# Layer 1's softmax sums: half of the queries added on GpSimd, the other half added later on DVE

## The chip, the cores and the metric

The kernel runs on one core of one Trainium2 chip. The metric is the device time of that core in microseconds (us), for the whole batch of eight samples. Engines are named as in the profile: PE is TensorE (PEld is its weight load), DVE is VectorE, ACT is ScalarE, POOL is GpSimd, SP is SyncE, whose queue issues the DMAs.

## The reference

Two attention blocks run one after the other on x of shape (8, 512, 32, 32), in f32. Layer 0 has eight heads and a group norm, layer 1 one head over all 512 channels and a norm over the whole sample. Layer 1, which is what the change touches, cut to what matters:

```python
n = (x - mean) * rsqrt(var + eps) * gamma + beta      # over c, h, w
q, k, v = wq @ n + bq, wk @ n + bk, wv @ n + bv        # (512, 1024) each
attn = softmax(einsum('bci,bcj->bij', q, k) * c ** (-0.5))   # 1024 queries x 1024 keys
out = einsum('bcj,bij->bci', v, attn)
return x + wo @ out + bo
```

## The kernel before

Each sample is worked off by itself: `layer0`, then `attention1`. The order on PE, ACT and DVE is the order in which the program is written (a manual schedule for these three engines); GpSimd and the DMA queue also follow that order as far as their own instructions go. Most matrix products are made in the Strassen-Winograd form, with seven products of quarters instead of eight, so that DVE has many additions of quarters: operands (names S1..S4 of the left side, T1..T4 of the right side) and results (a product in PSUM added to what is in SBUF).

`together(...)` runs several such products in turn, one step of each at a time, and `at_steps(steps, hooks)` puts extra work behind step n. So a hook's number sets where its instructions stand in the queues of DVE and ACT.

The scores of layer 1 are a matrix of 1024 keys by 1024 queries, held transposed in eight tiles `ps[j][k][i]`: j is the half of the keys, i the half of the queries, and k counts the two 256-key groups in a half. A tile is 128 partitions by 1024 f32 and holds two rows of 512 queries (index u). The scores go through two levels of Strassen-Winograd. At the outer level there are seven products: three (A11·B11, S2·T2, S3·T3) are made directly, by `line(t)` for each of four groups of 128 keys, and four are halved again by `twice(...)`: the local names are `p5`, `p2`, and then, in the last stage, the pair of `S4`·`B22` (queries half 0, keys half 1) and `A22`·`T4` (queries half 1, keys half 0). I call these two p3 and p4. Each `twice` has seven steps, each of one PE group of four 128x256 matmuls, and two PSUM banks, `line` and `single`: steps 1, 3, 5 and 7 write `line`, steps 2, 4 and 6 `single`. After each step DVE adds the bank to SBUF (`add`, L1143), or ACT copies it. Where the product is final, ACT takes the exponential of the finished quarter (`exp_of`, L1106).

The three stages of the scores stand in the code in this order:

1. `at_steps(together(line(0), p5, line(1), p5), {})`
2. `at_steps(together(line(2), p2, line(3), p2), {...})`, with hooks: `with_p5` (L1187) adds an outer product to a tile, `c22(k)` does this for tile `ps[1][k][1]` and takes its exponential, and `halve_a`, `halve_b` (L1036, L1044) make the operands for p4.
3. `with_p5(0, 1, 1)`, and p3 and p4 together, with `c22(1)` behind step 2.

The softmax denominators are sums of the exponentials over the keys. `add_up` adds the rows of the tiles of query half i into `acc[:, i, :]`, seven 128x512 additions for each half (L1101 the first, L1103 the others). In the kernel before each of them stands on DVE straight behind the exponential that it reads. Later `sums` (L1302) adds the partitions of `acc` by a matmul with ones, DVE takes the reciprocal, and a DMA spreads it.

Then `values(0)` and `values(1)` make the product with v in the Strassen-Winograd form over seven steps. `finish_values(n)` (L1233, L1237) makes operands S_n and T_n on DVE: n = 1 ahead of the first step, the others behind steps 1, 3 and 5; `sums` stands behind step 2. The first two products of each of `values(0)` and `values(1)` (A11·B11 and A12·B21) need no such operands.

PSUM has two buffers of tag `s` and two of tag `o`, which all these stages share in turn, so that a product can begin only when DVE or ACT has read what the last user of its buffer left.

Of the kernel before, what the change touches and what calls it, by code (L numbers as in the profile page):

```python
# [39 lines left out]
ALU = mybir.AluOpType  # L40
# [25 lines left out]
def two_attention_blocks(  # L66
# [17 lines left out]
    nc = tc.nc  # L84
# [13 lines left out]
    def banks(tag, name):  # L98
        return psum.tile([P, 2, HALF], FP, tag=tag, name=name)

    def tile2(name):
        return tpool.tile([P, 2, HALF], FP, tag="t", name=name)
# [351 lines left out]
    def together(*groups):  # L454

        groups = list(groups)
        spares.clear()
        while groups:
            for g in list(groups):
                if next(g, g) is g:  # L460
                    groups.remove(g)
                else:
                    yield
        spares.clear()

    def at_steps(steps, hooks):

        n = -1
        for n, _ in enumerate(steps):
            for hook in hooks.get(n, []):  # L470
                hook()
        assert n >= max(hooks, default=-1)
# [202 lines left out]
    def flat(t):  # L675
        return t.rearrange("p h n -> p (h n)")
# [322 lines left out]
    def attention1(xs, norm, b, at_values):  # L999
# [19 lines left out]
        def halve(part, order):  # L1019

            quarter = {}
            for i in range(2):
                for j in range(2):
                    k, n = order(i, j)
                    quarter[f"{i + 1}{j + 1}"] = part[:, k, n * 2 * P : (n + 1) * 2 * P]
            return quarter

        def halve_a(name):
            q = {f"A{n}": v for n, v in halve(q_parts[name], lambda i, j: (j, i)).items()}
            t = flat(tile2(f"{name}_twice_{b}"))  # L1030
            q.update({f"S{n + 1}": t[:, n * 2 * P : (n + 1) * 2 * P] for n in range(4)})
            for n, x, y, op in [
                (1, "A21", "A22", ALU.add), (2, "S1", "A11", ALU.subtract),
                (3, "A11", "A21", ALU.subtract), (4, "A12", "S2", ALU.subtract),
            ]:
                nc.vector.tensor_tensor(q[f"S{n}"], q[x], q[y], op)  # L1036
            twice_a[name] = q

        def halve_b(name):
            q = {f"B{n}": v for n, v in halve(bs[name], lambda i, j: (i, j)).items()}  # L1040
            t = flat(tile2(f"{name}_twice_{b}"))
            q.update({f"T{n + 1}": t[:, n * 2 * P : (n + 1) * 2 * P] for n in range(4)})
            for n, x, y in [(1, "B12", "B11"), (2, "B22", "T1"), (3, "B22", "B12"), (4, "B21", "T2")]:
                nc.vector.tensor_tensor(q[f"T{n}"], q[x], q[y], ALU.subtract)  # L1044
            twice_b[name] = q
# [48 lines left out]
        ps = [[[tile2(f"p_1_{b}_{j}{k}{i}") for i in range(2)] for k in range(2)] for j in range(2)]  # L1094
        acc = tile2(f"acc_1_{b}")
        seen = [[], []]

        def add_up(i, p):
            seen[i].append(p)
            if len(seen[i]) == 2:  # L1100
                nc.vector.tensor_tensor(acc[:, i, :], *seen[i], ALU.add)  # L1101
            elif len(seen[i]) > 2:
                nc.vector.tensor_tensor(acc[:, i, :], acc[:, i, :], p, ALU.add)  # L1103

        def exp_of(p):
            nc.scalar.activation(p, p, AF.Exp, scale=norm.factor)  # L1106

        def line(t):


            bank = banks("s", f"ps_s_1_{b}_{t}")[:, 0, :]
            for a, v, to in [
                ("A11", "B11", ps[0][t // 2][0]), ("S2", "T2", ps[1][t // 2][0]),
                ("S3", "T3", ps[0][t // 2][1]),
            ]:
                for k in range(2):
                    nc.tensor.matmul(  # L1117
                        bank, bs[v][:, k, t * P : (t + 1) * P], q_parts[a][:, k, :],
                        start=a == "A11" and k == 0, stop=k == 1, skip_group_check=True,
                    )  # L1120
                nc.scalar.copy(to[:, t % 2, :], bank)
                yield

        def twice(a, v, tags, i, j, fresh, final):

            a, v = twice_a[a], twice_b[v]
            line, single = (banks(tag, f"ps_{n}_1_{b}_{i}{j}")[:, 0, :] for tag, n in zip(tags, "ls"))

            def multiply(bank, x, y, start):
                for u in range(2):
                    nc.tensor.matmul(  # L1133
                        bank[:, u * 2 * P : (u + 1) * 2 * P], v[y][:, u * P : (u + 1) * P], a[x],
                        start=start and u == 0, stop=True, skip_group_check=True,
                    )

            def at(r, t):
                return ps[j][t][i][:, :, r * 2 * P : (r + 1) * 2 * P]

            def add(bank, r, t):
                bank = bank.rearrange("p (u q) -> p u q", u=2)
                nc.vector.tensor_tensor(at(r, t), bank, at(r, t), ALU.add)  # L1143

            def take(bank, r, t):
                if fresh:
                    nc.scalar.copy(at(r, t), bank.rearrange("p (u q) -> p u q", u=2))
                else:
                    add(bank, r, t)

            def done(r, t):
                if final:
                    exp_of(at(r, t))
                    if (r, t) in ((0, 1), (1, 0)):
                        for u in range(2):
                            add_up(i, ps[j][t][i][:, u, :])

            multiply(line, "A11", "B11", True)
            take(line, 0, 0)
            yield  # L1160
            multiply(single, "A12", "B21", True)
            add(single, 0, 0)
            done(0, 0)
            yield
            multiply(line, "S2", "T2", False)
            take(line, 0, 1)
            yield
            multiply(single, "S1", "T1", True)
            take(single, 1, 1)
            yield  # L1170
            multiply(line, "S3", "T3", False)
            add(line, 1, 1)
            done(1, 1)
            yield
            multiply(single, "S4", "B22", False)
            add(single, 0, 1)
            done(0, 1)
            yield
            multiply(line, "A22", "T4", False)
            take(line, 1, 0)  # L1180
            done(1, 0)
            yield

        def with_p5(i, j, k):

            to, other = ps[j][k][i], ps[1][k][1] if i == 0 else ps[0][k][1]
            nc.vector.tensor_tensor(to, to, other, ALU.add)  # L1187

        def c22(k):
            with_p5(1, 1, k)  # L1190
            exp_of(ps[1][k][1])
            for u in range(2):
                add_up(1, ps[1][k][1][:, u, :])

        p5 = twice("S1", "T1", "oo", 1, 1, True, False)
        at_steps(together(line(0), p5, line(1), p5), {})
        p2 = twice("A12", "B21", "oo", 0, 0, False, True)
        at_steps(together(line(2), p2, line(3), p2), {
            0: [lambda: with_p5(0, 1, 0)], 2: [lambda: c22(0)],
            6: [lambda: halve_a("A22")], 8: [lambda: halve_b("T4")],  # L1200
        })
        with_p5(0, 1, 1)
        at_steps(together(
            twice("S4", "B22", "so", 0, 1, False, True), twice("A22", "T4", "so", 1, 0, False, True)
        ), {2: [lambda: c22(1)]})

        tps = {f"T{n}": [tile2(f"t{n}_p_1_{b}_{k}") for k in range(2)] for n in range(1, 5)}
# [17 lines left out]
        def finish_values(n):  # L1225

            for k in range(2):
                a, b, a21, b12 = v_parts[k], p_parts[k], vs[k][:, :, 2 * P :], ps[0][k][1]
                x, y, op = {
                    1: (a21, a["A22"], ALU.add), 2: (a["S1"], a["A11"], ALU.subtract),  # L1230
                    3: (a["A11"], a21, ALU.subtract), 4: (a["A12"], a["S2"], ALU.subtract),
                }[n]
                nc.vector.tensor_tensor(a[f"S{n}"], x, y, op)  # L1233
                x, y = {
                    1: (b12, b["B11"]), 2: (b["B22"], b["T1"]), 3: (b["B22"], b12), 4: (b["B21"], b["T2"]),
                }[n]
                nc.vector.tensor_tensor(b[f"T{n}"], x, y, ALU.subtract)  # L1237
# [70 lines left out]
            invs.append(spread(invs[0], HD, lambda i: [(i, r) for r in range(2)], f"1_{b}"))  # L1308

        finish_values(1)  # L1310
        hooks = {n * 2 - 3: [lambda n=n: finish_values(n)] for n in range(2, 5)}
        hooks[5].extend([lambda: later.pop(0)()] * 2)
        hooks[2], hooks[6] = [sums], []
# [532 lines left out]
```

## Time and profile before

| | us |
|---|---|
| median of 3 runs | 2971.13 (2969.62 to 2971.99) |
| span of the profiled run | 2969.2 |
| PE busy | 2901.0 (98%) |
| DVE busy | 1944.7 (65%) |
| ACT busy | 1110.3 (37%) |
| POOL busy | 21.0 (1%), 28 instructions |
| mean granted PE clock | 0.986 of full speed |

PE is busy nearly all the time, so time can only go where PE idles (68.2 us of the span) or where it runs at less than its full clock. The busy share of PE says nothing of the second: a matmul at half the clock counts as busy for twice the time. The eight samples are alike; their periods are 365.2 us. The first samples' score stages begin near 320 and 686 us, the third's at 1051 us, and it is this third one that is read below.

### The profile page before, as it was taken

How to read it: one execution, taken by the hardware profiler on the slowest of the kernel's cores; microseconds unless marked ns; L12 is line 12 of the kernel's file. 1: busy time of each engine (PE TensorE's matmuls, PEld its weight loads, DVE VectorE, ACT ScalarE, POOL GpSimd, SP SyncE). 2: the span in 40 equal slices, each digit the busy share in tenths (PEclk: the TensorE clock that was granted, in tenths of full speed). 3: DMA queues.
4: the chain of work that ended last, by engine and by line, in shares of the span. 5: the costliest groups of instructions: out<-in, count | busy, mean ns of one | idle time of the engine just before them, and what ended most of it. 6: DMA issues, size and time to landing. Idle time of an engine off the chain costs nothing.

```text
span 2969.2 us, 35729 instructions
## 1 busy us (share of the span) xinstructions
PE 2901.0 (98%) x14480; PEld 1452.6 (49%) x14480; DVE 1944.7 (65%) x2580; ACT 1110.3 (37%) x1536; POOL 21.0 (1%) x28
## 2 busy tenths in 40 slices
PE   9999999999999999999999999999999999999998
PEld 6434654346533565335553355533555336553364
DVE  5676565765667656676566765677656775647846
ACT  3462314623155231552216522265222642226431
POOL 0000000000000000000000000000000000000000
PEclk9999999999999999999999999999999999999999
DMA  8412122220221203212032120322203222021001
GB/s 272 148 42 72 48 92 89 47 88 26 92 93 44 89 25 115 70 45 87 25 117 75 45 80 25 117 75 57 92 1 117 76 75 75 15 87 56 8 1 37
DMA packets 77661, 210.87 MB, mean 71 GB/s; under 512 B 19888, under 2 KB 20656, under 8 KB 71088
## 3 DMA queue, kind: packets, MB, share of 16 engines
q1 hardware_dynamic: 77344, 208.48, 22.1%
q8 instruction: 115, 1.88, 0.3%
q14 instruction: 58, 0.48, 0.1%
q10 hardware_dynamic: 144, 0.02, 0.0%
HBM read 137.43 MB, written 28.57 MB: 56 GB/s over the span
## 4 chain that ended last, share of the span: by engine, by line
PE 94%; DVE 4%; ACT 1%; issue 0%; POOL 0%; DVEq 0%; POOLq 0%
PE s L716 15%; PE ps_o L735 15%; PE ps_o L1245 14%; PE ps_q L479 13%; PE ps_v L494 13%; PE ps_k L479 7%; PE ps_p L479 6%; PE ps_s L1117 6%; PE ps_l L1133 2%; PE ps_s L1133 2%; DVE acc L1103 2%; DVE p L1143 1%; ACT p L1106 1%; DVE p L1187 1%; PE ps_wvo L596 0%; PE ps_wqk L626 0%
## 5 line engine op out<-in xcount | busy, mean ns | idle before, releaser
L645 ACT ACTIVATE p<-s 128x1024 f32<-128x1024 f32 x512 | 523.8, 1025 | 322.3 <-PE s L716 309.9
L647 DVE TENSOR_TENSOR acc<-acc,p 128x1024 f32<-128x1024 f32 x384 | 469.3, 1222 | 103.4 <-ACT p L645 92.0
L716 PE MATMUL s<-q,k 64*64 64x512 f32 x4096 | 531.5, 590 | 0.0
L735 PE MATMUL ps_o<-p,v 64*64 64x512 f32 x4096 | 528.7, 589 | 0.0
L716 PEld LDWEIGHTS s<-q,k 64*64 64x64 f32 x4096 | 154.0, 133 | 288.9 <-issue 266.0
L735 PEld LDWEIGHTS ps_o<-p,v 64*64 64x64 f32 x4096 | 156.6, 133 | 282.8 <-issue 278.0
L528 DVE TENSOR_TENSOR v<-ps_v,u_v 128x512 f32<-128x512 f32 x96 | 66.2, 690 | 164.4 <-PE ps_v L494 111.7
L421 ACT COPY u_v<-ps_v 128x512 f32<-128x512 f32 x96 | 56.3, 586 | 303.9 <-PE ps_v L494 295.3
L1245 PE MATMUL ps_o<-t_p,s_v 128*128 128x512 f32 x384 | 168.2, 594 | 0.0
L1245 PE MATMUL ps_o<-p,v 128*128 128x512 f32 x256 | 133.1, 686 | 31.2 <-DVE p L1143 31.2
L421 ACT COPY u_q<-ps_q 128x512 f32<-128x512 f32 x96 | 55.9, 582 | 250.3 <-PE ps_q L479 250.3
L1106 ACT ACTIVATE p<-p,factor 128x512 f32<-128x512 f32 (+1 forms) x112 | 87.2, 783 | 164.5 <-DVE p L1143 160.5
L647 DVE TENSOR_TENSOR acc<-p,p 128x1024 f32<-128x1024 f32 x64 | 77.9, 1217 | 84.6 <-ACT p L645 84.6
L1117 PE MATMUL ps_s<-s_q,t 128*128 128x512 f32 x256 | 120.3, 592 | 0.0
L1245 PEld LDWEIGHTS ps_o<-t_p,s_v 128*128 128x128 f32 x384 | 72.3, 190 | 94.5 <-issue 87.3
L479 PE MATMUL ps_q<-t,w_wqk 128*128 128x512 f32 x256 | 116.0, 597 | 0.0
L1143 DVE TENSOR_TENSOR p<-ps_l,p 128x512 f32<-128x512 f32 x104 | 69.8, 686 | 70.6 <-PE ps_l L1133 70.6
L479 PE MATMUL ps_p<-t_p,w_p 128*128 128x512 f32 x256 | 114.3, 595 | 0.6 <-DVE inv L658 0.5
L494 PE MATMUL ps_v<-w_wvo,t 128*128 128x256 f32 x512 | 113.1, 379 | 0.0
L856 DVE RECIPROCAL inv<-inv 128x512 f32<-128x512 f32 x28 | 93.7, 3346 | 22.9 <-ACT inv L654 22.9
L1245 PEld LDWEIGHTS ps_o<-p,v 128*128 128x128 f32 x256 | 56.0, 223 | 104.9 <-issue 104.9
L1143 DVE TENSOR_TENSOR p<-ps_s,p 128x512 f32<-128x512 f32 x88 | 59.9, 687 | 71.1 <-PE ps_s L1133 71.1
(318 smaller groups left out, 4043.8 us busy)
## 6 DMA issues: line engine op xcount, KB each, us to landing
x<-in_x SPq DMA_DIRECT2D x92, 512.0 KB, 7.2
w_qk<-stored_qk SPq DMA_DIRECT2D x14, 1792.0 KB, 7.2
inv<-inv SPq DMA_DIRECT2D x248, 64.0 KB, 2.0
w_wqk<-stored_wqk SPq DMA_DIRECT2D x8, 1792.0 KB, 8.2
fold<-acc SPq DMA_DIRECT2D x56, 256.0 KB, 3.1
w_wvo<-stored_wvo SPq DMA_DIRECT2D x8, 1792.0 KB, 7.7
out<-x SPq DMA_DIRECT2D x28, 512.0 KB, 2.8
w_v<-stored_v SPq DMA_DIRECT2D x7, 1792.0 KB, 7.0
```

The source lines that it names most:

```text
L421: nc.scalar.copy(us[n][:, :width], line[:, :width])
L479: nc.tensor.matmul(bank, w[a][:, k, c * P : (c + 1) * P], bs[b][:, k, :], start=fresh and k == 0, stop=k == 1, skip_group_check=True,)
L494: nc.tensor.matmul(bank[:, u * 2 * P : (u + 1) * 2 * P], bs[b][:, k, n * P : (n + 1) * P], w[a][:, k, :], start=fresh and u == k == 0, sto ...
L645: nc.scalar.activation(p, s, AF.Exp, scale=factor)
L647: nc.vector.tensor_tensor(acc, first, p, ALU.add)
L716: nc.tensor.matmul(s[cols, j, :], flat(ks[pair])[rows, k0 : k0 + HD], qs[pair][rows, g, :], start=True, stop=True,)
L735: nc.tensor.matmul(o[cols, half, :], vs[kt][rows, c0 : c0 + HD], p[rows, j, :], start=kt == 0, stop=kt == NT - 1,)
L1106: nc.scalar.activation(p, p, AF.Exp, scale=norm.factor)
L1117: nc.tensor.matmul(bank, bs[v][:, k, t * P : (t + 1) * P], q_parts[a][:, k, :], start=a == "A11" and k == 0, stop=k == 1, skip_group_check ...
L1133: nc.tensor.matmul(bank[:, u * 2 * P : (u + 1) * 2 * P], v[y][:, u * P : (u + 1) * P], a[x], start=start and u == 0, stop=True, skip_group ...
L1143: nc.vector.tensor_tensor(at(r, t), bank, at(r, t), ALU.add)
L1245: nc.tensor.matmul(bank, v_parts[kt // 2][a][:, kt % 2, c * P : (c + 1) * P], p_parts[kt // 2][b][:, kt % 2, cols], start=fresh and kt == ...
```

## The change

`add_up` gets the tile's indices in place of a row, and the engine is chosen by the half of the queries: half 0 on GpSimd, straight behind the exponentials as before; half 1 on DVE, but no longer behind the exponentials. One of its four tiles is added behind step 10 of stage 2, the other three after `finish_values(1)`, ahead of the first product with v. Further, in stage 2 the hooks move up: `c22(0)` from step 2 to 1, `halve_a("A22")` from 6 to 4, `halve_b("T4")` from 8 to 6, and `with_p5(0, 1, 1)` goes from behind the stage into its step 8. The order on PE is the same, instruction by instruction. The purpose is that DVE doesn't wait for exponentials between the additions for which PE waits.

```diff
-        def add_up(i, p):
-            seen[i].append(p)
-            if len(seen[i]) == 2:
-                nc.vector.tensor_tensor(acc[:, i, :], *seen[i], ALU.add)
-            elif len(seen[i]) > 2:
-                nc.vector.tensor_tensor(acc[:, i, :], acc[:, i, :], p, ALU.add)
+        def add_up(j, k, i):
+
+            engine = nc.vector if i else nc.gpsimd
+            for u in range(2):
+                seen[i].append(ps[j][k][i][:, u, :])
+                if len(seen[i]) == 2:
+                    engine.tensor_tensor(acc[:, i, :], *seen[i], ALU.add)
+                elif len(seen[i]) > 2:
+                    engine.tensor_tensor(acc[:, i, :], acc[:, i, :], seen[i][-1], ALU.add)
...
-                    if (r, t) in ((0, 1), (1, 0)):
-                        for u in range(2):
-                            add_up(i, ps[j][t][i][:, u, :])
+                    if i == 0 and (r, t) in ((0, 1), (1, 0)):
+                        add_up(j, t, i)
...
             exp_of(ps[1][k][1])
-            for u in range(2):
-                add_up(1, ps[1][k][1][:, u, :])
...
-            0: [lambda: with_p5(0, 1, 0)], 2: [lambda: c22(0)],
-            6: [lambda: halve_a("A22")], 8: [lambda: halve_b("T4")],
+            0: [lambda: with_p5(0, 1, 0)], 1: [lambda: c22(0)], 4: [lambda: halve_a("A22")],
+            6: [lambda: halve_b("T4")], 8: [lambda: with_p5(0, 1, 1)], 10: [lambda: add_up(1, 0, 1)],
         })
-        with_p5(0, 1, 1)
...
         finish_values(1)
+        for j, k in [(1, 1), (0, 1), (0, 0)]:
+            add_up(j, k, 1)
```

## The prediction

> **What bounds the kernel now.** I first read the page's busy shares (PE 98%), then the list of waits for PE alone, because only what makes PE wait can be worth anything. It is short:
>
> ```profile
> PE ps_o L1245 <- DVE p L1143: 31.2, 8, 3.9
> PE ps_l L1133 <- DVE p L1143: 20.0, 8, 2.5
> PE ps_s L1133 <- DVE p L1143: 9.8, 8, 2.7
> ```
>
> That is 61.0 of PE's 68.2 us of idle time: three waits per sample (2.5, about 1.2, and 3.9 us), all for DVE's additions of score products. Next, the table of stages for the third sample: stages 1 and 2 of the scores; stage 3; the first four products with v; the rest of those; everything else of the period.
>
> ```profile
> 1051.20:1083.90 32.70, 32.70 (x105) 19.77 (x105) 12.68 (x21) 11.76 (x19) 0.00 (x0) 1.00 0.15 56
> 1083.90:1105.80 21.90, 14.50 (x57) 11.49 (x57) 17.09 (x26) 6.96 (x10) 0.00 (x0) 0.89 0.00 1
> 1105.80:1122.30 16.50, 16.49 (x33) 7.18 (x34) 7.54 (x10) 2.51 (x4) 0.00 (x0) 0.84 0.00 0
> 1122.30:1158.00 35.70, 35.70 (x86) 15.47 (x85) 30.84 (x37) 6.70 (x12) 0.00 (x0) 1.00 0.33 104
> 1158.00:1416.40 258.40, 258.40 (x1512) 124.73 (x1512) 172.42 (x222) 109.27 (x144) 2.42 (x2) 1.00 0.25 77
> ```
>
> The columns are stretch, length, busy time of PE, PEld, DVE, ACT, POOL, and then PE's clock. Everywhere but in the second and third row PE is busy throughout at clock 1.00. In stage 3 it is busy for 14.50 of 21.90 us, at 0.89, and in the next row, where it doesn't wait, the clock is 0.84. So each stall costs twice: the wait, and a slow time after it. The weight loads show the slow time directly, at the start of the values and a little later:
>
> ```profile
> 1106.80 0.34 PEld L1245 LDWEIGHTS ps_o<-p,v 128*128 128x128 f32 x1 [0.52 <-issue]
> 1107.65 0.34 PEld L1245 LDWEIGHTS ps_o<-p,v 128*128 128x128 f32 x1 [0.52 <-issue]
> ...
> 1111.99 0.19 PEld L1245 LDWEIGHTS ps_o<-p,v 128*128 128x128 f32 x1 [0.24 <-issue]
> 1112.42 0.19 PEld L1245 LDWEIGHTS ps_o<-p,v 128*128 128x128 f32 x1 [0.24 <-issue]
> ```
>
> One every 0.85 us, then one every 0.43: half speed until 1111.5. Last, the chain of waits says what DVE does while PE stands:
>
> ```profile
> 1099.36 0.70 DVE p L1143
> 1100.06 0.02 issue
> 1100.08 0.73 ACT p L1106
> 1100.81 0.02 issue
> 1100.84 0.70 DVE acc L1103
> 1101.54 0.02 issue
> 1101.56 0.69 DVE acc L1103
> 1102.26 0.61 DVE p L1143
> ```
>
> An addition, its exponential, two sums that wait for it (0.78 us in which DVE stands), and only then the next addition, that PE needs. This round takes 2.8 us; PE makes the group for the next addition in 0.86.
>
> **What the Trainium skill says.** (1) "TensorE: Matmul & The Clock Gate", Part 1 (the HAM clock gate): PE drops to half its clock after an idle window of about 3.4 us and needs about as long a busy one to return; the windows run freely. The trace agrees in kind: half speed behind the 2.5 and 3.9 us waits, none behind the 1.0 us wait. (2) "SBUF — State Buffer", "Who interferes with whom": a DVE instruction with two SBUF inputs contends with a GpSimd instruction that reads SBUF, and the second to issue waits for the first; one with a single SBUF input doesn't. No run here shows it yet, GpSimd being idle at this place. (3) "GPSIMD Engine Reference", 3.1: a GpSimd f32 add of two tensors of 2048 elements takes 4497 ns, 1.96 times DVE's.
>
> **The change, part by part.**
>
> *The sums leave stage 3.* DVE's timeline has the 14 sums of this sample at 0.69 us each: one in stage 2 (1073.75), nine in stage 3 (1084.75 to 1105.1), four behind it. The nine go, 6.2 us, and with them DVE's waits for their exponentials (0.79 us each where the line of ACT is free, 1.21 at 1093.53). What stays is 14 additions at a pitch of 0.60 us (two back to back: 1084.75 to 1085.35) and one `with_p5` at 1.14: 9.5 us, against 14 PE groups x 0.86 = 12.04 us. So DVE becomes the faster of the two, and PE should run through. I walked it by hand with the delays of the trace: an addition starts 1.06 us after its PE group (1082.20 to 1083.26), and PE resumes 0.06 us after an addition (1089.98 to 1090.04).
>
> The last two groups of p2 start at 1082.20 and 1083.06, as before; additions at 1083.26 and 1084.12. p3 and p4 then start a group every 0.86 us from 1083.93. Additions: p3's first at 1084.99, p4's first 1085.85, p3's second 1086.71, then `with_p5(1, 1, 1)` 1087.31 to 1088.54, p4's second 1088.45 to 1089.14. PE needs: for p3's third group (1087.38) p3's first addition, ended 1085.68; for p4's third (1088.24) 1086.54; for p3's fourth (1089.10) 1087.40; for p4's fourth (1089.96) 1089.14. All are in time, the tightest by 0.8 us. From there DVE gains 0.26 us per addition. p3's last starts about 1095.3 and ends 1096.0; PE comes to the values, which take over that bank, at 1095.98. Start of the values: 1096.0 in place of 1105.81, **9.8 us earlier**.
>
> *The slow clock.* With PE never idle, the first four products with v run at 0.43 us for each of 32 matmuls: 13.76 us in place of 16.48 (1105.81 to 1122.29), **2.7 us**. The half-speed groups of stage 3 are inside the 9.8.
>
> *Hooks of stage 2.* `c22(0)` a step sooner doesn't change DVE's order, only ACT's: its exponential (1.15 us) stands ahead of a copy that then ends near 1073.9; PE needs that bank at 1075.32. The operands for p4 and `with_p5(0, 1, 1)` (1.23 us) lie in DVE gaps of this stage (DVE busy 12.68 of 32.70). The one early sum (0.69) at step 10 fits between additions at 1080.7 and 1083.3. Cost nothing: PE, at clock 1.00 there, hides them.
>
> *Six sums on DVE behind `finish_values(1)`.* 6 x 0.72 = 4.3 us behind operands that can begin when p4's last exponential ends, near 1097.6: operands until 1101, sums until 1105.5. Behind them on DVE is the addition of `values(0)`'s first result, ready at 1103.1; PE reuses that bank for S1·T1 only at 1109.8. Hidden, with 3.6 us to spare. `finish_values(2)` follows the second such addition (1110 to 1114) and PE wants it at 1117.5.
>
> *Seven sums on GpSimd.* The trace has no such add there; its only two-tensor operations are 128x4 and 128x1 powers of 1.02 and 1.40 us. Lower bound: the skill's 4497/2048 x 512 = 1.1 us. Upper: that plus a fixed 1.4 us = 2.5. I take 1.2. Three run from 1084.8, four from about 1096.1: done by 1101 alone, or near 1106 if DVE's two-input additions push in between. PE's `sums` wants them at 1096.0 + 13.76 + 3.44 = 1113.2. Hidden up to 4.2 us for one add.
>
> *What GpSimd takes from DVE.* In stage 3 a single DVE instruction has two SBUF inputs, `with_p5(1, 1, 1)` at 1087.3, when GpSimd's third sum may be in flight. It can be held by one add, 0 to 1.2 us (2.5 at the upper price), against 0.8 us of slack: 0 to 0.4 us of stall (1.7 at most). I take 0.4.
>
> Sum: 9.8 + 2.7 - 0.4 = 12.1 us per sample. The waits are alike in all eight (each line counts 8), so 8 x 12.1 = 97 us: 2971.1 - 97 = **2874 us**.
>
> **Rivals.**
> - *Contention brings back a stall.* For it: the port rule above, and a GpSimd price not measured here. At 2.5 us an add, 1.7 us of stall; if that also drops the clock, as the 2.5 us wait did, some 2 us more, and the 12.5 shrinks to 8.8: 2971 - 70 = 2901. Against: the other DVE additions of the stage have one SBUF input (the other is PSUM). I give it 0.12, for 2885 to 2925.
> - *GpSimd is late, and PE waits in `sums` instead.* It needs over 4.2 us for one add. At 5 us: 3.2 us of wait and some 2.7 of slow clock, 12.1 becomes 6.2: 2921. Against: over four times the page's rate. 0.03.
> - *Slower than before.* GpSimd at 8 us an add, or DVE blocked for most of its two-input work: 15 us of wait at `sums` and 2.7 of slow clock against 12.5 saved, 5 us lost per sample: 3012. Against: the same rate, and PE's stall, which is in the chain of waits, is taken away in any case. 0.04. About no change, 0.02, would need wait and gain to meet.
>
> **Numbers.** The forecast's own case, PE running through but for a fraction of a us, has 0.79: 2866 to 2882 (0 to 1 us of stall per sample, and some 4 us for a first sample that waits 2.7 us where the others wait 1.0). The range 2864 to 2892 adds the mild end of the first rival, and leaves out under 0.2. Faster by over 0.2%: 0.94.
>
> **What would show it.** Right: the three waits of PE gone or under 1 us each; stage 3 about 12 us with clock near 1.00, also in the stretch behind it; POOL busy up by 56 adds; DVE's busy time down by 56 x 0.69 = 39 us; mean clock near 1.00. Wrong step by step: a wait of PE for DVE with `with_p5` held (contention), a wait at `sums` for POOL (price), or the slow clock at the start of the values without a wait ahead of it.

## The result, and the profile after

2871.66 us (median of four runs, 2871.3 to 2871.9) against 2971.56 us for the kernel before beside it: ratio 0.966, 95% interval 0.965 to 0.968. That is 99.9 us less; the forecast was 2874.

The list of waits for PE, of the changed kernel, is the first thing to compare with before:

```profile
PE ps_warm L1351 <- POOL in_sample L163: 1.2, 1, 1.2
PE ps_p L479 <- DVE inv L658: 0.6, 1, 0.6
PE ps_wvo L596 <- DMA wo<-in_w_o: 0.2, 1, 0.2
```

The three lines with 61.0 us are gone, and nothing came in their place in the scores and values. The table of stages of the changed kernel, again for the third sample and cut at the same places of the program (stages 1 and 2; stage 3; the values' first four products; the rest of the values; the rest of the period):

```profile
1025.20:1057.90 32.70, 32.70 (x106) 19.77 (x105) 13.84 (x22) 11.76 (x19) 0.00 (x0) 1.00 0.15 56
1057.90:1069.90 12.00, 12.00 (x57) 10.44 (x55) 10.35 (x16) 6.82 (x9) 5.46 (x4) 1.00 0.01 1
1069.90:1083.70 13.80, 13.79 (x34) 6.17 (x33) 11.95 (x13) 2.62 (x4) 5.55 (x4) 1.00 0.00 1
1083.70:1119.40 35.70, 35.70 (x85) 15.33 (x85) 30.83 (x37) 6.80 (x12) 0.00 (x0) 1.00 0.32 103
1119.40:1378.10 258.70, 258.70 (x1513) 124.91 (x1512) 172.35 (x222) 109.22 (x144) 2.49 (x2) 1.00 0.25 77
```

Row 2 went from 21.90 to 12.00 us, row 3 from 16.50 to 13.80, each now with PE busy throughout at clock 1.00. The other rows are as they were, within 0.3 us. So the whole gain of a sample, 12.3 us (period 365.2 to 352.9), lies in the two rows of the prediction.

The timelines of DVE and of POOL in stage 3 and at the start of the values (start, length, engine and line; in brackets the idle time before) show what took the place of the rounds of addition, exponential and sums. DVE:

```profile
1060.68 0.69 DVE L1146 TENSOR_TENSOR p<-ps_s,p 128x512 f32<-128x512 f32 x1 [0.17 <-PE ps_s L1136]
1061.29 1.22 DVE L1189 TENSOR_TENSOR p<-p,p 128x1024 f32<-128x1024 f32 x1
1062.42 0.68 DVE L1146 TENSOR_TENSOR p<-ps_s,p 128x512 f32<-128x512 f32 x1
1063.02 1.28 DVE L1146 TENSOR_TENSOR p<-ps_l,p 128x512 f32<-128x512 f32 x2
1064.21 1.47 DVE L1146 TENSOR_TENSOR p<-ps_s,p 128x512 f32<-128x512 f32 x2
1065.86 0.69 DVE L1146 TENSOR_TENSOR p<-ps_l,p 128x512 f32<-128x512 f32 x1 [0.17 <-PE ps_l L1136]
...
1070.78 1.57 DVE L1232 TENSOR_TENSOR s_v<-v,v 128x512 f32<-128x512 f32 x1
1072.27 2.28 DVE L1236 TENSOR_TENSOR t_p<-p,p 128x1024 f32<-128x1024 f32 x1
1074.48 1.75 DVE L1232 TENSOR_TENSOR s_v<-v,v 128x512 f32<-128x512 f32 x1
1076.15 1.21 DVE L1236 TENSOR_TENSOR t_p<-p,p 128x1024 f32<-128x1024 f32 x1
1077.29 4.31 DVE L1106 TENSOR_TENSOR acc<-acc,p 128x512 f32<-128x512 f32 x6
1081.51 0.68 DVE L1257 TENSOR_TENSOR u_o<-ps_o,u_o 128x512 f32<-128x512 f32 x1
```

POOL:

```profile
1058.75 1.28 POOL L1104 TENSOR_TENSOR acc<-p 128x512 f32<-128x512 f32 x1 [67.75 <-ACT p L1109]
1060.11 3.53 POOL L1106 TENSOR_TENSOR acc<-acc,p 128x512 f32<-128x512 f32 x2
1069.17 6.51 POOL L1106 TENSOR_TENSOR acc<-acc,p 128x512 f32<-128x512 f32 x4 [5.54 <-ACT p L1109]
```

In stage 3 DVE works off its additions and from 1065.86 on stands idle 0.17 us before each: now it waits for PE. Further down one sees the contention: while GpSimd makes its last four sums (1069.17 to 1075.68), DVE's operands with two SBUF inputs take 1.57, 2.28 and 1.75 us, where the kernel before has 0.68, 1.22 and 0.68; the fourth, behind GpSimd's end, takes 1.21, as before. All this ends before PE asks for it.

### The profile page after: what moved, and what is told of

It reads as the page before. It is cut to its first block, busy times and chain, and to the rows that moved or that the text cites. A ratio compares the mean times of both kernels' runs of the same rounds, so it can differ in the third digit from the quotient of the medians.

```text
span 2869.6 us, 35809 instructions
## 1 busy us (share of the span) xinstructions
PE 2861.8 (100%) x14480; PEld 1436.3 (50%) x14480; DVE 1934.8 (67%) x2524; ACT 1110.3 (39%) x1536; POOL 109.5 (4%) x84
## 4 chain that ended last, share of the span: by engine, by line
PE 98%; DVE 1%; SPq 0%; DMA 0%; issue 0%; ACT 0%; DVEq 0%; ACTq 0%
PE s L716 15%; PE ps_o L735 15%; PE ps_v L494 13%; PE ps_q L479 13%; PE ps_o L1244 13%; PE ps_k L479 7%; PE ps_p L479 6%; PE ps_s L1120 6%; PE ps_l L1136 4%; PE ps_s L1136 3%; PE ps_wvo L596 0%; PE ps_wqk L626 0%; DVE inv L658 0%; PE ps_o L1301 0%; DVE acc L647 0%; PE ps_sum L844 0%
## 5 line engine op out<-in xcount | busy, mean ns | idle before, releaser
L1244 PE MATMUL ps_o<-p,v 128*128 128x512 f32 x256 | 111.8, 594 | 0.1
L1124 ACT COPY p<-ps_s 128x512 f32<-128x512 f32 x96 | 56.1, 584 | 125.6 <-PE ps_s L1120 124.5
```

Source lines behind the costliest of these rows:

```text
L1244: nc.tensor.matmul(bank, v_parts[kt // 2][a][:, kt % 2, c * P : (c + 1) * P], p_parts[kt // 2][b][:, kt % 2, cols], start=fresh and kt == ...
```

## The experiments

My theory was that the sums' place in DVE's queue cost the time: DVE works in order, so a sum that waits for its exponential holds up the addition behind it, for which PE waits. Rivals: DVE simply had too much work; the moved hooks did it; GpSimd's help did it. Time, PE's waits for DVE or ACT in the scores and values (the sum of the listed waits, eight samples) and PE's mean granted clock in the profiled run of each kernel:

| kernel | us (median of 4 runs; `e3` of 20) | ratio to before, 95% | PE's waits there, us | clock |
|---|---|---|---|---|
| before | 2971.6 | | 61.0 | 0.986 |
| changed | 2871.7 | 0.965 to 0.968 | 0 | 1.0 |
| e1, all sums on DVE, 13 of 14 late | 2877.7 | 0.967 to 0.970 | 2.8 | 1.0 |
| e2, half 0 on GpSimd alone | 2946.9 | 0.990 to 0.994 | 47.6 | 0.99 |
| e3, hooks alone | 2965.4 | 0.997 to 0.999 | 63.7 | 0.989 |
| e4, sums that wait for nothing | 2915.0 | 0.979 to 0.982 | 34.1 | 0.997 |
| e5, sums moved, hooks of before | 2874.6 | 0.966 to 0.969 | 0 listed | 1.0 |
| e6, short delay put in | 2890.8 | 0.971 to 0.974 | 15.1 | 0.998 |
| e7, long delay put in | 2938.1 | 0.987 to 0.990 | 46.1 | 0.991 |
| e8, half 0 on DVE in place | 2901.7 | 0.975 to 0.978 | 24.4 | 1.0 |
| e9, `with_p5` a step sooner | 2872.9 | 0.965 to 0.969 | 0 | 1.0 |
| e10, all sums on GpSimd | 2871.4 | 0.965 to 0.968 | 0 | 0.999 |

### Waiting or work: e4

```diff
         def add_up(i, p):
+            p = vs[len(seen[i]) // 2][:, len(seen[i]) % 2, :]
             seen[i].append(p)
```

> The kernel before, with each sum in its place on DVE but adding a row of v, which is ready long before, in place of the exponentials: same work, no wait for ACT (the denominators are then not those of the softmax). My theory in its two parts: the waits for exponentials go, the 0.6 to 0.7 us of each sum stay ahead of the additions; DVE has about 14 x 0.60 + 2 x 1.14 + 9 x 0.61 = 16 us for a stage that PE makes in 12. About 2944 us: a third of the gain. Rival (all of it is work): 2965 to 2972 us. Rival (all of it is waiting): 2871 to 2880 us.

Measured: 2915.0 us. Of the 99.9 us, 56.6 go when the sums no longer wait, with DVE's instructions, their number and order unchanged; 43.3 are left (some 3 of them the hooks', by `e5` below), so neither rival holds. PE's waits of `e4`:

```profile
PE ps_o L1246 <- DVE p L1144: 17.1, 8, 2.1
PE ps_s L1134 <- DVE p L1144: 11.2, 8, 1.4
PE ps_l L1134 <- DVE p L1144: 5.8, 8, 0.7
```

Two of the three waits are shorter by 1.8 us each (3.9 to 2.1, 2.5 to 0.7), the third is about as long (1.2 and 1.4). What is left comes mostly from the sums' own time ahead of the additions. I had put waiting at a third of the gain; it is 57%. One reason is the clock: I had counted slow time behind the last wait of each sample, but of the eight samples' first 32 matmuls with v only four were slowed, by 1.7 us each. Between the profiled runs of the two kernels the clock record's half-speed time falls from 81.9 to 13.7 us; worked out from it and from the starts of PE's groups, about half of the 54 us between their spans is clock and half is PE's idle time. More on this at e6 and e7.

### Which move matters: e2, e8, e3, e5

`e2` takes the engine change for half 0 alone; half 1 and the hooks are as before:

```diff
-                    if i == 0 and (r, t) in ((0, 1), (1, 0)):
+                    if (r, t) in ((0, 1), (1, 0)):
...
             exp_of(ps[1][k][1])
+            add_up(1, k, 1)
...
-            0: [lambda: with_p5(0, 1, 0)], 1: [lambda: c22(0)], 4: [lambda: halve_a("A22")],
-            6: [lambda: halve_b("T4")], 8: [lambda: with_p5(0, 1, 1)], 10: [lambda: add_up(1, 0, 1)],
+            0: [lambda: with_p5(0, 1, 0)], 2: [lambda: c22(0)],
+            6: [lambda: halve_a("A22")], 8: [lambda: halve_b("T4")],
         })
+        with_p5(0, 1, 1)
...
-        for j, k in [(1, 1), (0, 1), (0, 0)]:
-            add_up(j, k, 1)
```

> Half 0 on GpSimd, half 1 on DVE straight behind its exponentials as before, hooks as before. My theory: the six sums of half 1 still stand in stage 3 and wait for exponentials, so most of PE's waits stay, at other places: about 2969 us (2940 to 2975). Rival (half of the sums gone from DVE gives half of the gain or more): 2921 us or less.

`e8` does the opposite: half 1 late as in the change, half 0 back on DVE behind its exponentials.

```diff
-            engine = nc.vector if i else nc.gpsimd
+            engine = nc.vector
```

> The changed kernel with half 0's sums on DVE in place of GpSimd, at the same place, straight behind their exponentials; half 1 late as in the change. My theory: seven sums with their waits stand in stage 3 and just ahead of the values: about 4.6 us of PE wait and some 3 us of slow clock per sample, 2935 us (2915 to 2955). Rival (it was enough to move half 1): 2871 to 2885 us.

Measured: 2946.9 and 2901.7 us. `e2`, with half of the sums off DVE, gains 24.7 us, a quarter; two waits of 2.7 and 3.3 us per sample stay. Moving half 1, with the hooks, gains 69.9 (`e8`). The two add up to 94.6 of 99.9. Both rivals fall: half of the sums isn't half of the gain, and it wasn't enough to move half 1. Both times came out shorter than I expected. For `e2` (2969; 2946.9 is still in its range) more of the wait went than I had thought: 47.6 us are listed, where the kernel before has 61.0, and half-speed time fell too, from 81.9 to 58.0 us. `e8` lies outside its range (2915 to 2955): I had counted 4.6 us of wait and 3 us of slow clock per sample, but 3.05 are listed, and its clock record shows no half speed in any sample.

`e3` moves the hooks alone, in the kernel before:

```diff
-            0: [lambda: with_p5(0, 1, 0)], 2: [lambda: c22(0)],
-            6: [lambda: halve_a("A22")], 8: [lambda: halve_b("T4")],
+            0: [lambda: with_p5(0, 1, 0)], 1: [lambda: c22(0)], 4: [lambda: halve_a("A22")],
+            6: [lambda: halve_b("T4")], 8: [lambda: with_p5(0, 1, 1)],
         })
-        with_p5(0, 1, 1)
```

> The kernel before with the hooks of the changed one, sums where they were. My theory: nothing gained, since the sums still stand between the additions; with_p5(0, 1, 1) leaves stage 3 (1.1 us less there), but a sum that waits for c22(0)'s exponential stands in stage 2: 2960 to 2990 us. Rival (sooner operands are what helps): 2871 to 2920 us.

`e5` is the counterpart: the changed kernel with the hooks of before.

```diff
-            0: [lambda: with_p5(0, 1, 0)], 1: [lambda: c22(0)], 4: [lambda: halve_a("A22")],
-            6: [lambda: halve_b("T4")], 8: [lambda: with_p5(0, 1, 1)], 10: [lambda: add_up(1, 0, 1)],
+            0: [lambda: with_p5(0, 1, 0)], 2: [lambda: c22(0)],
+            6: [lambda: halve_a("A22")], 8: [lambda: halve_b("T4")],
+            10: [lambda: add_up(1, 0, 1)],
         })
+        with_p5(0, 1, 1)
```

> The changed kernel with the hooks of before (operands and with_p5(0, 1, 1) where they were); only the sums move. My theory: with_p5(0, 1, 1) takes 1.14 us of DVE at the start of stage 3 and shifts the additions for p3 and p4; 0.8 us of wait per sample at most: 2872 to 2880 us, about 2878. Rival (the moved hooks carry a good part of the gain): over 2890 us.

Measured: 2965.4 us for the hooks alone (6 us faster), 2874.6 us for the sums alone (97 us faster). So, with the sums moved, the moved hooks are worth 3 us and the sums all the rest. The 6 us of the hooks alone are no shorter wait: 63.7 us are listed, against 61.0. They lie in the clock, whose half-speed time is 64.9 us there and 81.9 before. The timeline of `e5` shows where part of the 3 us sits: `with_p5(1, 1, 1)` is held by a GpSimd sum there, 1.85 us long, and the PE group that waits for the addition behind it starts 0.2 us late.

### Is GpSimd needed: e1 and e10

`e1` puts all 14 sums on DVE; the one behind step 10 of stage 2 stays there, the other 13 are late:

```diff
-            engine = nc.vector if i else nc.gpsimd
+            engine = nc.vector
...
-                    if i == 0 and (r, t) in ((0, 1), (1, 0)):
-                        add_up(j, t, i)
...
         for j, k in [(1, 1), (0, 1), (0, 0)]:
             add_up(j, k, 1)
+        for j, k in [(0, 1), (0, 0), (1, 1), (1, 0)]:
+            add_up(j, k, 0)
```

> All 14 sums of a sample on DVE and none on GpSimd; those of half 0 stand behind those of half 1, after finish_values(1). My theory (the sums' place in DVE's queue cost the time: waits for exponentials and work ahead of additions for which PE waits): DVE has 13 x 0.72 = 9.4 us of sums in the stretch of the values' first four products, which is 13.8 us; the first result of the values is then added about 0.6 us later than PE wants its bank. About 2877 us, 0 to 1.5 us of PE wait per sample. Rival (GpSimd's help is what counts, DVE hasn't the time for 14 sums anywhere): the wait moves into the values, several us per sample, 2900 to 2970 us.

`e10` puts all 14 on GpSimd, at the places of the changed kernel:

```diff
-            engine = nc.vector if i else nc.gpsimd
+            engine = nc.gpsimd
```

> All 14 sums on GpSimd, at the places of the changed kernel. If GpSimd's own time stays hidden: ten sums from about 10.5 us behind the start of stage 3 at 1.3 to 2.2 us each end 24 to 32 us behind it, and PE wants them at 29.6: between 2872 us (no wait) and 2890 us (2 us of wait). Rival (contention with DVE's operands delays the values): DVE's finish_values held by more than its 3.6 us of slack, over 2890 us.

Measured: 2877.7 and 2871.4 us. With no GpSimd at all, 94 of the 99.9 us are there; PE then waits in the values for the late addition of the first result, as its list of waits says:

```profile
PE ps_o L1242 <- DVE u_o L1255: 2.8, 8, 0.4
```

So what counts is that the sums leave their place; GpSimd saves the last 6 us, most of them this wait (0.35 us listed per sample, about 0.52 from group to group): DVE has no room for all 13 in the values' first four products. With all sums on GpSimd the time is that of the changed kernel (the two differ by 0.2 us), though GpSimd works until 12 us into the values. Neither GpSimd's time nor its contention reaches PE.

### The contention: e9

```diff
-        ), {2: [lambda: c22(1)]})
+        ), {1: [lambda: c22(1)]})
```

> The changed kernel with c22(1) behind step 1 of stage 3 in place of step 2, so that with_p5(1, 1, 1), the one DVE instruction of the stage with two SBUF inputs, comes up in the middle of a GpSimd sum. If it is held until that sum ends (about 1 us): p3's second addition is late, 0.3 to 1 us of PE wait per sample, 2874 to 2880 us, and with_p5 shows over 1.22 us. If GpSimd is held in its place: 2872 us, no wait, GpSimd's sum about 1 us longer.

Measured: 2872.9 us (2872.1 to 2873.8), 1.2 us above the changed kernel, and no wait of PE in the scores or values in the list; where the 1.2 us lie is not shown. The timeline of DVE in `e9`:

```profile
1059.88 0.69 DVE L1146 TENSOR_TENSOR p<-ps_l,p 128x512 f32<-128x512 f32 x1 [0.17 <-PE ps_l L1136]
1060.49 2.02 DVE L1189 TENSOR_TENSOR p<-p,p 128x1024 f32<-128x1024 f32 x1
1062.44 1.28 DVE L1146 TENSOR_TENSOR p<-ps_s,p 128x512 f32<-128x512 f32 x2
```

`with_p5` (L1189), which took 1.22 us in the changed kernel, takes 2.02: it came up while a GpSimd sum was under way (begun at 1060.17, 1.27 us alone) and ended about 1.1 us behind that one's end. So DVE is held, as the Trainium skill says ("SBUF — State Buffer", "Who interferes with whom"). In the changed kernel the same instruction came up at 1061.29, when the sum begun at 1060.11 was all but over, and it was GpSimd's next sum that was held: 2.18 us, the longest there, in place of 1.27. (In `e9` GpSimd's next sum is held as well, behind `with_p5`: 2.13 us.) Whether `with_p5` is held is a matter of 0.8 us of timing. I had expected 0.3 to 1 us of PE wait if it is; the slack absorbed it.

### The slow clock: e6 and e7

Both are the changed kernel with reciprocals that nobody uses, on DVE ahead of the last addition for p3:

```diff
+    idle = const.tile([P, 32], FP, tag="idle", name="idle")
...
-        ), {2: [lambda: c22(1)]})
+        ), {2: [lambda: c22(1)], 11: [lambda: nc.vector.reciprocal(idle, ones[:, :32])] * 6})
```

and `* 16` in `e7`.

> The changed kernel with six reciprocals of 128x32, about 0.26 us each, which nobody uses, on DVE behind step 11 of stage 3, ahead of the addition for which the values' first product waits: a PE wait of known place, about 1.4 us per sample. My theory of the slow clock (it comes behind a wait of some 2.5 us or more): 8 x 1.4 = 11 us, 2883 us, and clock 1.00 in the values' first stretch. Rival (any wait slows what follows): 8 x (1.4 + 2.7), 2904 us.

> The same with sixteen reciprocals, about 4.2 us: a PE wait of about 4 us per sample, as long as the one at this place before the change. With the slow clock as before: 8 x (4.0 + 2.7) = 54 us, 2925 us, and clock near 0.84 in the values' first four products. Rival (the slow clock before the change came from the three waits together, or from the products themselves): 8 x 4.0 = 32 us, 2904 us.

Measured: 2890.8 and 2938.1 us. A reciprocal took 0.38 us and not 0.26, so the waits are 1.9 and 5.8 us, longer than forecast, and so are both times (2883 and 2925). In `e7` the time rose by 66.4 us, of which 46.1 are the listed waits; in all eight samples the 32 matmuls behind them took 15.4 to 17.0 us where they take 13.97 without a wait. So a single wait brings the slow clock, without the two earlier ones and in the same products. In `e6` it rose by 19.1, of which 15.1 are waits, and here the samples differ. Two of them in the timeline of PE of `e6` (length of the 32 matmuls; in brackets the wait ahead of them):

```profile
1432.61 15.67 PE L1245 MATMUL ps_o<-p,v 128*128 128x512 f32 x32 [1.89 <-DVE p L1147]
...
2833.74 13.97 PE L1245 MATMUL ps_o<-p,v 128*128 128x512 f32 x32 [1.89 <-DVE p L1147]
```

The same wait, and one sample runs on at full speed, the other 1.70 us slower. So neither my theory (slow behind 2.5 us or more) nor its rival (any wait slows) holds. What decides is how much of the wait falls into one step of a fixed grid, as the clock record of the traces shows: within a run the clock changes only at points of one even grid of 3.41 us, and each of the 56 half-speed stretches of all runs is one or two steps of it long. These are steps of that grid in `e6`, two at the wait of the slow sample and three at that of the fast one (the columns are those of the table of stages):

```profile
1429.35:1432.76 3.41, 1.52 (x8) 1.04 (x7) 3.24 (x9) 1.25 (x3) 2.53 (x2) 1.00 0.00 0
1432.76:1436.18 3.42, 3.42 (x5) 1.36 (x6) 3.21 (x4) 1.07 (x2) 2.74 (x2) 0.50 0.00 0
2828.81:2832.23 3.42, 3.04 (x15) 2.33 (x13) 2.97 (x7) 2.44 (x4) 1.27 (x1) 1.00 0.00 0
2832.23:2835.64 3.41, 1.90 (x5) 0.97 (x6) 3.13 (x7) 1.33 (x2) 2.41 (x2) 1.00 0.03 5
2835.64:2839.05 3.41, 3.41 (x10) 1.50 (x9) 3.41 (x3) 0.58 (x1) 2.40 (x2) 1.00 0.00 0
```

In the slow sample the whole wait lies in one step, where PE is busy for 1.52 us only, and the next step runs at half speed. In the fast sample the same wait is cut by the grid, 0.4 and 1.5 us, and no step follows at half speed.

## Why the prediction was right

*Start of the values, 9.8 us sooner.* Right in size: in the changed kernel PE comes to them 12.26 us behind the start of stage 3 (1057.89 to 1070.15), the walk gave 12.0; 0.18 us is the hand-over of the bank at the end, for which the walk had next to nothing (1095.98 to 1096.0). DVE did become the faster engine of the two. What the walk could not say is how the gain divides; `e4` says it: 57 us go with the waiting, and 43 us with the work, the place and the hooks.

*The slow clock, 2.7 us.* Right: 16.64 to 13.97 us in the timeline of the 32 matmuls. `e7` shows that it follows from the wait ahead. As a rule for the experiments, though, "slow behind 2.5 us" was too simple: it depends on where in the clock's grid the wait falls (`e6`), and the 2.5 us wait of the first sample, which the grid cut into 1.35 and 1.32 us, was followed by no half speed. In all, by an estimate from the clock record and the starts of PE's groups, the clock is 35 of the 99.6 us between the profiled spans (half of the 70 us that PE worked at half speed before), and PE's idle time is the other 64. Of the clock's share, what falls in stage 3 is inside the 9.8.

*Hooks at no cost.* Right: stages 1 and 2 take 32.70 us as before. That they are worth 3 us was not forecast.

*Six sums on DVE behind the operands.* Hidden, but with less to spare than I had: the operands were held by GpSimd and ended 7.2 us behind the values' start (I had 5), the sums 11.5 us behind it (9.5), and the addition of the first result at 1082.2, where PE wants the bank at 1083.95: 1.8 us in place of 3.6. Operands held by GpSimd was the term I left out of this step.

*Seven sums on GpSimd.* 1.27 us for one alone, one every 1.35, where I took 1.2; 1.6 in the mean with what holds them. Done 5.5 us into the values, and 11.8 us before PE's `sums` wants them. That this is close to the walk without contention (5) is luck: the four were held, 6.51 us in place of 4.8, but began 1.0 us ahead of the values and not with them.

*The stall by contention, 0.4 us per sample.* Wrong: none there, as GpSimd and not DVE was held (none of the eight took over 1.23 us). That was close, as `with_p5` came up about 0.1 us before GpSimd's second sum ended; so it is in part luck. In `e9` being held for 0.8 us cost no listed wait; in `e5`, where the instruction stood later in the stage, 0.6 us of it cost 0.2. The two gains before it had summed to 12.5 us; 12.3 were measured, 12.1 forecast. Eight times 12.3 is 98.4 us, and the spans differ by 99.6: the first sample, whose wait had been 2.7 us where the others had 1.0, gave the rest. These two make 2.8 us; the gain was 99.9 us where 97 were forecast.

*DVE's busy time down by 39 us.* Wrong as a sign to look for: it fell by 9.9 (1944.7 to 1934.8). A held instruction counts as busy, 3.0 us per sample in the three operands alone, and additions that used to overlap back to back now stand apart.

## What to carry to other kernels

In an engine that works in order, a short instruction that waits costs what stands behind it: look first at whether the instruction for which the bound engine waits sits behind one that nobody waits for, and move that one, to any place where its wait is over. Which engine it goes to matters less (94 of 100 us came without GpSimd). And count a stall of PE with what the clock takes afterwards; the busy share of PE hides that part, the clock column shows it.

## What the runs showed of the hardware that was not expected

Whether a wait of PE brings the slow clock looks like chance whose odds rise with the wait's length: of eight samples, the 32 matmuls behind the wait were slowed in none at 1.69 us (`e8`), two at 1.89 (`e6`), four at 2.14 (`e4`), all eight at 3.27 (`e2`), all eight at 3.90 in the kernel before but seven in `e3`, and all eight at 5.77 (`e7`). Within a run it is not chance. I estimate PE's idle time in each step of the 3.41 us grid, from the gaps between PE's groups and 0.17 us more for each (see below), over the twelve profiled runs. At full speed, all 51 steps with 2.19 us or more of it were followed by half speed, none of the 66 with 1 to 2.00 us was, and of nine between these five were. At half speed, the clock stayed so for another step behind all 25 steps with 0.66 us or more of idle time, and came back behind all 56 with 0.59 or less. So the one wait of 3.90 us with no slow time behind it (`e3`) is no exception: the grid cut it into 2.13 and 1.94 us. Where the grid lies against the program differs from run to run (in the four runs of `e4` the mean clock was 0.997 to 0.999), so that a kernel with such waits also spreads more: 2962 to 2968 us in the twenty runs of `e3`.

The Trainium skill ("TensorE: Matmul & The Clock Gate", Part 1) gives a free-running window of 3413 ns, and the grid of the traces agrees with that length. It lets the clock drop after an idle window; here a window with 2.2 of its 3.41 us idle was enough, and the measurement decides.

The list of waits shows each wait of PE some 0.17 us too short. It counts from the end that the profile models for a group, 1.03 us behind its start, while groups without a wait follow each other every 0.86 us: in `e4` a group started at 1073.62, the next began at 1075.38, which is 0.90 us of gap, and 0.73 is listed. Small waits drop out of the list altogether: the 0.2 us in `e5` is not in it.
